# Placing eight batches of scan states on the 128 partitions: two row layouts for broadcast DMAs

## The chip, the cores and the metric

The kernel runs on one core of one Trainium2 chip. The metric is the device time of one execution in microseconds, the median over repeated runs. The core has five engines that follow their own instruction streams: TensorE (PE in the profile, with its weight loads as PEld), VectorE (DVE), ScalarE (ACT), GpSimd (POOL) and SyncE (SP). SP does no arithmetic here; it issues every DMA of the kernel. The transfers themselves are done by 16 DMA engines, which the core's queues share.

## The reference, cut to what matters

Input x is 8 batches of 1024 positions of 512 channels. Two residual layers follow each other: a modulated attention with 16 heads, and a gated state-space scan. Only the scan is touched. With 1024 inner channels, 16 states per batch and position t, it computes

```
xr, gate = split(x @ W_in.T);  xc = silu(conv4(xr + t_emb));  xn = layernorm(xc) * ln_g + ln_b
Bm, Cm, dt = split(xn @ W_xproj.T);  dt = tanh(dt @ W_dt.T + b_dt) * 0.01
ad = 1 + dt * (-tanh(A_log));  bd = Bm * min(norm(xn), 1)
h[b, n, :] = clip(h[b, n, :] * ad[b, n] + bd[b, n] * xn[b, t, :], -10, 10)      # for each t
y[b, t, :] = sum over n of Cm[b, n] * h[b, n, :]
out = x + ((y + D * xn) * silu(gate)) @ W_out.T
```

The state h is therefore 8 x 16 = 128 rows of 1024 channels: one row per partition. At each position all 16 rows of a batch need the same vector xn[b, t, :].

## The kernel before, in words

The attention fills the first 3.5 ms and hands its result to the scan through DRAM. The scan takes positions in 32 chunks of 32 (`TC`), each made of two tiles of 16 positions (`TT`). In a tile the 128 partitions hold (position, batch) pairs for the layer norm; for the recurrence the 128 partitions hold (state, batch) pairs. The change of layout is a round trip through DRAM, on the SP queue:

- `spill` (L622) writes the normalised tile `xt`, 128 x 1024, to a DRAM tile `xd`, 512 KB, ordered so that the 4 positions x 1024 channels that one batch needs next lie together, 16 KB. Its DRAM side has the shape 4 x 32 x 1024, its SBUF side 128 x 1024.
- `fetch` (L765) reads back four positions at a time. For each of the eight batches it issues one DMA that reads one 16 KB piece and writes it to that batch's 16 partitions, `xb[rows(b)]`: eight broadcasts of 256 KB, 2 MB in all, per four positions. The tiles `xb` have three buffers of four positions.
- `rows(b)` (L514) says which partitions those are. Before, batch b has the partitions 64*(b//4) + b%4 + 4n for the states n = 0 to 15: batches 0 to 3 lie interleaved in partitions 0 to 63, batches 4 to 7 in partitions 64 to 127. The broadcasts are issued in the order 0, 4, 1, 5, 2, 6, 3, 7, which alternates between the halves.

`spread` (L665) uses the same `rows(b)` for eight small DMAs per chunk that bring the recurrence's coefficients from 16 partitions to 128 (`bca`). The rest of the recurrence is one instruction per position and engine: ACT multiplies `xb` by a column of weights (`weigh`, L779, in place), DVE adds it to the state and saturates (`step`, L802, tile `h`, six buffers), and after four positions PE forms the outputs with the matrices `yw` (`products`, L784). `yw` is the coefficient times `mask_y`, which is 1 where a partition belongs to a batch; that matrix and the columns `b_dt` and `a_log` are laid out on the host.

Everything is issued in an order written out by hand. `at(n, f, ...)` puts a piece of work at step n, where one step is one position; at every step the recurrence comes first and then the pieces in the order in which they were put there. For chunk c, with p0 = 32(c-1), the first tile's spill stands at step p0+17 and the second's at p0+21; `skip` (L636), which multiplies `xt` in place and so must wait until the spill has read it, stands at p0+20 and p0+26. `fetch(g)` stands at step 4g-9, `weigh(n)` two steps ahead of position n, `products(g)` at 4g+4. All engines work their streams in order. SP also waits in order: each DMA carries one of eight semaphores in turn, so that a DMA is issued only once the one eight places ahead of it has landed.

Also on the SP queue in each chunk: a load of `x1` (512 KB, L435) and eight stores of the output (`out_send`, L755, 64 KB each, whose DRAM side is 4 x 8 x 512).

Of the kernel before, what the change touches and what calls it, by code (L numbers as in the profile page):

```python
# [15 lines left out]
P = 128  # L16
B = 8
# [6 lines left out]
NS = 16  # L24
TC = 32
TT = 16
EPS = 1e-5
EPS_DM = 1e-8


@with_exitstack
def modulated_attention(ctx, tc, const, x1_d, xu_d, S, x, xT, cond, wT, ident, sT):
# [80 lines left out]
    with tc.tile_pool(name="w0", bufs=2) as wp:  # L113
        s2T = wp.tile([P, 2 * KH, B], F32, name="s2T")
        nc.scalar.activation(s2T, sT, AF.Square)
        for n, name in enumerate(NAMES):
# [5 lines left out]
            for o in range(KH):  # L122
                for k in range(KH):
# [6 lines left out]
                    )  # L130
            nc.vector.tensor_scalar_add(dc[:, n], d_ps, EPS_DM)
        nc.scalar.activation(dc, dc, AF.Sqrt)
# [266 lines left out]
def gated_scan(ctx, tc, const, x1_d, S, w_in, w_conv, cols, ln_g, ln_b, w_x, w_xd, w_dt, b_dt, a_log,  # L399
# [113 lines left out]

    def rows(b):  # L514

        r0 = 64 * (b // 4) + b % 4
        return slice(r0, r0 + 4 * (NS - 1) + 1, 4)

    def by_rows(ap):

# [144 lines left out]
    def spread(st):  # L665
        st["bca"] = one.tile([P, 3, TC], F32, name="bca")
        for b in range(B):
            nc.sync.dma_start(out=st["bca"][rows(b)], in_=xp[:, :, b, :])
# [96 lines left out]
    def fetch(g):  # L765

        c, t = divmod(4 * g, TC)
        i, q = divmod(t // 4, TT // 4)
        xb = xbp.tile([P, 4, DI], F32, name="xb")
        for b in (0, 4, 1, 5, 2, 6, 3, 7):  # L770
            src = sts[c]["xd", i].rearrange("(q b) r c -> q b (r c)", q=4)[q, b]
            nc.sync.dma_start(  # L772
                out=xb[rows(b)].rearrange("p r c -> p (r c)"),
                in_=src.unsqueeze(0).to_broadcast([NS, 4 * DI]),
            )
        for r in range(4):
            xbs[4 * g + r] = xb[:, r]
# [86 lines left out]
    for g in range(S // 4):  # L864
        at(4 * g - 9, fetch, g)
        at(4 * g + 4, products, g)
# [99 lines left out]
```

## Time and profile before

| what | us |
| --- | --- |
| median of 3 runs (6273.12 to 6277.6) | 6274.84 |
| the profiled execution's own time | 6262.97 |
| its span in the profile | 6261.2 |
| scan, from the first broadcast to the last state | about 3536 to 6240 |
| PE busy in the stretch 3560 to 6240 | 2447.53 of 2680 |
| DVE busy there | 2243.25 |
| ACT busy there | 1912.92 |
| mean busy share of the 16 DMA engines there | 0.82 |
| data moved there | 224 GB/s |

PE's busy time counts pipelined matmuls with modelled ends. The DMA share is the mean over 16 engines, so it can hide that a few of them carry more than the rest. One chunk of 32 positions takes 2680/32 = 83.75 us. The attention before it is not touched by the change.

### The profile page before, as it was taken

What the parts mean: (1) busy time and instruction counts of PE and PEld (TensorE: products, weight loads), DVE (VectorE), ACT (ScalarE), POOL (GpSimd) and SP (SyncE); (2) the same over time, 40 slices, a digit from 0 to 9 for tenths busy, and PEclk for the clock granted to TensorE, in tenths of its full rate; (3) what the DMA queues carried; (4) which work ended last, traced back from release to release, by engine and by line L of the source; (5) the groups of instructions that cost most, each with busy time, mean ns of one, the idle gap of its engine ahead of it and who ended that gap; (6) DMA issues with size and microseconds to landing.
All of it is one profiled execution on the core that took longest, in us unless ns stands there. A gap on an engine that the chain in (4) does not pass through costs nothing.

```text
span 6261.2 us, 112973 instructions
## 1 busy us (share of the span) xinstructions
PE 5796.5 (93%) x42960; PEld 3314.5 (53%) x42960; DVE 4484.0 (72%) x6917; ACT 3843.8 (61%) x6743; POOL 1266.2 (20%) x1156
## 2 busy tenths in 40 slices
PE   7999999999999999999999699999999999999998
PEld 5555555655555555555555444444444444444443
DVE  2666666656667666666665488888888888888887
ACT  3555655655556556555554477777777777677675
POOL 2433433434334334343332000000000000000000
PEclk8999999999999999999999899999999999999999
DMA  2112111112121111121211678888888888888787
GB/s 70 35 30 71 30 55 49 35 48 67 30 70 31 55 48 35 48 67 30 55 28 55 177 224 223 221 221 228 225 223 227 222 222 228 220 224 226 221 223 198
DMA packets 396859, 781.65 MB, mean 125 GB/s; under 512 B 196496, under 2 KB 295056, under 8 KB 363552
## 3 DMA queue, kind: packets, MB, share of 16 engines
q1 hardware_dynamic: 396320, 774.44, 45.4%
q8 instruction: 341, 5.59, 0.4%
q14 instruction: 198, 1.62, 0.1%
HBM read 663.62 MB, written 83.89 MB: 119 GB/s over the span
## 4 chain that ended last, share of the span: by engine, by line
PE 60%; DMA 14%; DVE 10%; ACT 8%; SPq 5%; issue 3%; POOL 0%; DVEq 0%; ACTq 0%; POOLq 0%
PE mm_ps L153 16%; PE t_ps L262 13%; PE s_ps L252 9%; DMA xb<-xd 8%; PE mm_ps L269 8%; DVE h L806 5%; DMA xd<-xt 4%; PE o_ps L745 4%; SPq L772 4%; PE in_ps L547 4%; ACT pr L370 3%; PE y_ps L793 3%; ACT pT L367 1%; PE g_ps L705 1%; PE in_ps L551 1%
## 5 line engine op out<-in xcount | busy, mean ns | idle before, releaser
L360 DVE TENSOR_REDUCE nmax<-s_ps 128x1 f32<-128x1024 f32 x1024 | 1206.2, 1220 | 478.0 <-PE s_ps L255 477.4
L806 DVE CUSTOM_DVE_ANT_0 h<-h,xb,lim 128x1024 f32<-128x1024 f32 x1024 | 1374.7, 1342 | 209.7 <-PE y_ps L793 71.7
L367 ACT COPY pT<-t_ps 128x512 f32<-128x512 f32 x1024 | 549.8, 589 | 1378.8 <-PE t_ps L262 1378.5
L262 PEld LDWEIGHTS t_ps<-ident,pr 128*128 128x128 f32 x8192 | 909.7, 141 | 646.4 <-issue 453.2
L782 ACT ACTIVATE xb<-xb,ws 128x1024 f32<-128x1024 f32 x1024 | 1135.9, 1145 | 62.4 <-DVE ws L682 31.3
L370 ACT ACTIVATE pr<-s_ps,nmax 128x1024 f32<-128x1024 f32 x1024 | 1139.6, 1127 | 6.1 <-DVE nmax L360 5.7
L262 PE MATMUL t_ps<-ident,pr 128*128 128x128 f32 x8192 | 1096.1, 277 | 30.7 <-ACT pT L367 28.5
L793 PE MATMUL y_ps<-h,yw 128*32 128x512 f32 x4096 | 675.5, 617 | 159.7 <-DVE h L806 159.6
L252 PE MATMUL s_ps<-kT,qT 32*128 32x512 f32 x2048 | 601.1, 641 | 4.4 <-ACT pr L370 4.4
L389 POOL TENSOR_SCALAR pr<-pr,rinv 128x1024 f32<-128x1024 f32 x512 | 572.6, 1118 | 145.6 <-DVE rinv L388 142.9
L255 PE MATMUL s_ps<-k,q 32*128 32x512 f32 x2048 | 578.2, 640 | 0.0
L269 PEld LDWEIGHTS mm_ps<-pT,vt 128*32 128x32 f32 x16384 | 438.0, 110 | 235.1 <-issue 94.3
L705 PE MATMUL g_ps<-win,x1t 128*128 128x512 f32 x1024 | 508.5, 643 | 58.1 <-ACT sq_ps L631 51.3
L269 PE MATMUL mm_ps<-pT,vt 128*32 128x128 f32 x16384 | 517.6, 274 | 47.5 <-ACT vt L200 18.5
L547 PE MATMUL in_ps<-x,win 128*128 128x256 f32 x2048 | 490.9, 383 | 28.9 <-ACT xt L733 17.4
L375 POOL TENSOR_SCALAR pr<-pr,rinv 128x1024 f32<-128x1024 f32 x256 | 286.5, 1119 | 1109.5 <-PE t_ps L262 741.0
L547 PEld LDWEIGHTS in_ps<-x,win 128*128 128x128 f32 x2048 | 389.8, 192 | 152.4 <-issue 71.6
L384 POOL TENSOR_SCALAR pr<-pr,rinv 128x1024 f32<-128x1024 f32 x256 | 286.3, 1118 | 882.6 <-DVE rinv L383 855.8
L745 PE MATMUL o_ps<-wout,xt 128*128 128x512 f32 x1024 | 463.7, 596 | 0.7 <-ACT xt L733 0.7
L793 PEld LDWEIGHTS y_ps<-h,yw 128*32 128x32 f32 x4096 | 133.9, 110 | 545.6 <-DVE h L806 295.0
L381 DVE COPY pT<-t_ps 128x512 f32<-128x512 f32 x512 | 352.2, 688 | 77.2 <-PE t_ps L262 76.8
L705 PEld LDWEIGHTS g_ps<-win,x1t 128*128 128x128 f32 x1024 | 198.2, 204 | 384.6 <-issue 229.5
(129 smaller groups left out, 6750.7 us busy)
## 6 DMA issues: line engine op xcount, KB each, us to landing
xb<-xd SPq DMA_DIRECT2D x2048, 256.0 KB
xd<-xt SPq DMA_DIRECT2D x64, 512.0 KB
xq<-in_x SPq DMA_DIRECT2D x16, 1024.0 KB
q<-qT SPq DMA_DIRECT2D x128, 128.0 KB
xr<-in_xT SPq DMA_DIRECT2D x64, 256.0 KB
xu_d<-xr SPq DMA_DIRECT2D x64, 256.0 KB
xr<-xu_d SPq DMA_DIRECT2D x64, 256.0 KB
x_d<-xr SPq DMA_DIRECT2D x64, 256.0 KB
```

What stands on the lines that cost most here:

```text
L153: nc.tensor.matmul(ps, w, x, start=(k == 0), stop=(k == KH - 1))
L252: nc.tensor.matmul(s_ps[i][:, 0:HW], st["q"][r, qc], st["k"][r, 0:HW], start=True, stop=True)
L262: nc.tensor.transpose(ps[:, j], pr[:, c0 : c0 + P], ident)
L269: nc.tensor.matmul(av[r], vt[:, kt, r], pT[:, i, kt], start=(kt == 0), stop=(kt == KT - 1), skip_group_check=True,)
L360: nc.vector.tensor_reduce(nmax[i], s_ps[i], AX.X, ALU.max, negate=True)
L370: nc.scalar.activation(fresh[i], s_ps[i], AF.Exp, bias=nmax[i], accum_out=rsum[i])
L547: nc.tensor.matmul(ps, win_sb[:, kk, k * P : (k + 1) * P], st["x1"][:, kk].rearrange("p b t -> p (b t)"), start=(kk == 0), stop=False,)
L705: nc.tensor.matmul(ps, st["xo", i][:, k], win_sb[:, k, DI + half * 512 : DI + (half + 1) * 512], start=(k == 0), stop=(k == KH - 1),)
L745: nc.tensor.matmul(ps, st["gT", i][:, k, :], wout_sb[:, k, :], start=False, stop=(k == KI - 1), skip_group_check=True,)
L782: nc.scalar.mul(xbs[n], xbs[n], sts[c]["ws"][:, t : t + 1])
L793: nc.tensor.matmul(st["y", i][32 * r : 32 * r + 32, hf * 512 : (hf + 1) * 512], yws[i][:, 4 * q + r, :], hs[4 * g + r][:, hf * 512 : (hf + ...
L806: nc.vector._custom_dve(dve_ops.TENSOR_ADD_SAT, out=h, in0=last["h"], in1=xbs.pop(n), s0=lim[:, 0, t : t + 1], s1=lim[:, 1, t : t + 1],)
```

## The change

The partitions of a batch are given by a new function. Batches 0 to 3 now have the partitions 32 + b + 4n, that is the middle half 32 to 95, four batches interleaved. Batches 4 and 5 have b%2 + 2n, the first quarter 0 to 31, two batches interleaved; batches 6 and 7 have 96 + b%2 + 2n, the last quarter 96 to 127. The order in which the eight broadcasts of a group are issued becomes 4, 6, 0, 1, 5, 7, 2, 3. The host lays out `mask_y`, `b_dt` and `a_log` by the same function.

```diff
+def state_rows(b):
+
+    if b < B // 2:
+        return 32 + b, 4
+    return 96 * (b // 6) + b % 2, 2
...
     def rows(b):
 
-        r0 = 64 * (b // 4) + b % 4
-        return slice(r0, r0 + 4 * (NS - 1) + 1, 4)
+        r0, d = state_rows(b)
+        return slice(r0, r0 + d * (NS - 1) + 1, d)
...
-        for b in (0, 4, 1, 5, 2, 6, 3, 7):
+        for b in (4, 6, 0, 1, 5, 7, 2, 3):
...
-    mask_y = np.broadcast_to(
-        np.eye(B, dtype=np.float32).reshape(2, 1, 4, B), (2, NS, 4, B)
-    ).reshape(P, B)
+    batch_of, state_of = np.zeros(P, int), np.zeros(P, int)
+    for b in range(B):
+        r0, d = state_rows(b)
+        batch_of[r0 + d * np.arange(NS)] = b
+        state_of[r0 + d * np.arange(NS)] = np.arange(NS)
+    mask_y = np.eye(B, dtype=np.float32)[batch_of]
...
     def rows(v):
-        return np.tile(np.repeat(np.asarray(v), 4), 2)[:, None]
+        return np.asarray(v)[state_of][:, None]
```

The number of instructions, their order on each engine, their sizes and what each waits for stay as they are.

## The prediction

> **What bounds the kernel now.** I began with the page's slices, which split the run at about 3.5 ms into attention and scan.
>
> ```profile
> DMA  2112111112121111121211678888888888888787
> GB/s 70 35 30 71 30 55 49 35 48 67 30 70 31 55 48 35 48 67 30 55 28 55 177 224 223 221 221 228 225 223 227 222 222 228 220 224 226 221 223 198
> ```
>
> In the scan the DMA engines are busy for eight tenths. Only the scan uses the changed rows, so the first 3.5 ms cannot move. Next, the chain of waits over the scan alone (3555 to 6240 us), by line:
>
> ```profile
> by line: DMA xb<-xd 18.7%; DVE h L806 11.8%; DMA xd<-xt 9.5%; PE o_ps L745 9.5%; SPq L772 8.5%; PE in_ps L547 7.9%; PE y_ps L793 6.4%; issue 4.4%; PE g_ps L705 2.8%; PE o_ps L739 1.9%; PE in_ps L551 1.9%; ACT xb L782 1.9%; DVE xt L605 1.7%;
> ```
>
> Broadcasts in flight hold 18.7% of 2685 us = 502 us of the chain, spills in flight 9.5% = 255 us. Then the list of waits over 3560 to 6240, for what the lateness does:
>
> ```profile
> ACT sq_ps L631 <- DVE xt L620: 238.0, 32, 8.8
> ...
> PE y_ps L793 <- DVE h L806: 159.6, 105, 3.1
> ...
> DVE xt L637 <- DMA xd<-xt: 127.4, 58, 4.3
> ...
> DVE h L806 <- ACT xb L782: 55.2, 67, 2.7
> ...
> PE g_ps L705 <- ACT sq_ps L631: 51.3, 28, 3.7
> ```
>
> DVE stands 127 us on spills, since `skip` may not overwrite `xt` before the spill has read it; behind it in DVE's order stand the scaling (L620) and the states. PE then waits 160 us for states and 51 us for the squares behind L620. PE idles 2680 - 2447.53 = 232 us in the scan, mostly for a late DVE. That is the most that any faster transfer can give.
>
> Last, how fast transfers run by the partitions that they write, from five short stretches. The last two columns are the DMA share and GB/s.
>
> ```profile
> 679.10:680.10 1.00, 1.00 (x9) 1.00 (x10) 0.57 (x3) 0.77 (x3) 0.00 (x0) 1.00 0.95 207
> 3471.00:3473.00 2.00, 0.00 (x0) 0.00 (x0) 0.00 (x0) 0.00 (x0) 0.00 (x0) 0.50 1.01 416
> 3480.00:3481.50 1.50, 0.00 (x0) 0.00 (x0) 0.00 (x0) 0.00 (x0) 0.00 (x0) 0.50 1.00 399
> 5009.00:5013.00 4.00, 4.00 (x13) 2.17 (x12) 4.00 (x5) 2.71 (x4) 0.00 (x0) 1.00 0.99 266
> 5130.00:5130.80 0.80, 0.80 (x5) 0.17 (x1) 0.25 (x1) 0.00 (x0) 0.00 (x0) 0.50 0.25 102
> ```
>
> Row 1 is a copy of 64 partitions to the other 64 in the attention (L177, L178): every DMA engine busy, 207/0.95 = 218 GB/s. Row 2 is the load of `win` to 128 partitions, 416/1.01 = 412. Row 3 is mostly the broadcasts of layer-norm rows and D to 128 partitions: one 4 KB source read 128 times, yet 399. Row 4 is a stretch of nothing but broadcasts to `xb`: 266/0.99 = 269. Row 5 is a spill alone: a quarter of the engines, 102 GB/s.
>
> [...]
>
> [...]
>
> **The change part by part.** Sizes from the issue list: a broadcast has 256 KB = 262144 B.
>
> *Broadcasts now.* 262144/269 = 0.975 us each; eight make 7.80 us, and a chunk of eight groups 62.4 us on each engine. Engines 0 to 3 add two spills of 524288/102 = 5.14 us each, eight output stores of eight 2 KB pieces per engine (84 ns each in the packet records, 0.67 us a store), and the `x1` load of 524288/412 = 1.3 us: 62.4 + 10.3 + 5.4 + 1.3 = 79.4 us of 83.75, 95%. The other twelve carry 63.7 us. The mean, (4 x 79.4 + 12 x 63.7)/16 = 67.6, is 0.81 of a chunk, against the 0.82 measured: the working holds. Four DMA engines are thus the fullest resource, above PE's 91%.
>
> *Broadcasts after.* Batches 0 to 3: 262144/412 = 0.636 us. For 4 to 7 the trace has no case [...]: at best they go as now (0.975; they still come in pairs from both sides, 4-6 and 5-7), at worst as row 1 (1.20). Eight cost 2.54 + 3.90 = 6.44 us, or 7.35 us. I take 6.44: the alternation that gives 269 is kept. That is -1.36 us per group (-17%), with -0.45 us (-6%) as the weak end. Engines 0 to 3 fall to 68.5 us, 82%, per chunk.
>
> *What of it lies on the path.* Pieces of broadcast flight on the chain are 6.0 us long on average, so 502/6.0 = 84 of them. About 2.0 us is fixed (at the scan's first broadcast 1.35 us from issue to the first packet, and 0.65 us from a packet's end to its semaphore); 4.0 us is queue. At 17% that saves 0.7 us; engines at 82% instead of 95% also keep a shorter queue, for which I add 0.3 as an estimate. 84 x 1.0 = 84 us. Spill pieces average 10.26 us, 255/10.26 = 25: 2.0 fixed, 5.14 own transfer, unchanged, and 3.1 behind the group issued just ahead. Taking a third of that, 1.1, gives 25 x 1.1 = 28 us. Together 112 us. A quarter I count as taken over by what is late next and sees no DMA: DVE waiting for PE at the states (72 us) and at the statistics (71 us). That leaves -84 us.
>
> *At no cost.* The order of the eight issues: as many, each about 0.63 us of SP; a batch issued first isn't used earlier, since `weigh` reads all 128 partitions and waits for the last. The small `bca` DMAs (6 KB) change partitions only; they stand under `decay` three steps (8 us) later, and if that cover were gone their eight issues would cost 5 us a chunk, as before. `mask_y` and columns: host layout, same loads. No wait is added; `skip`, and DVE's work behind it, keeps the same wait for an earlier landing.
>
> Sum: 6262.97 - 84 = 6179 for the profiled execution; the shown runs lie 12 us above it, hence 6274.84 - 84 = about 6190.
>
> **The rivals.**
>
> *Slower: engines 0 to 3 collide with each other.* [...] with only four engines in a broadcast, packets took 0.61 us. [...] 32 x 0.636 + 32 x 1.20 = 58.8 us; if one packet in eight then takes 1.8, 63 us or more, above today's 62.4. It decides once their mean packet passes 0.975 us. At +0.3 us for 84 pieces: +25 us, 6300. Against: with twelve engines active, packets cluster near 0.92 us, 12 x 16 KB at 213 GB/s, not at 0.61 for four and 1.20 for eight. The half seems to be shared evenly.
>
> *No change: the source is the limit.* 269 could be what sixteen readers of one DRAM piece get. Then it stays at 6275. Row 3 speaks against it (one source, 399), and row 1 shows the half's limit with no DRAM at all.
>
> *Small gain: the weak end.* 7.35 us per group, or PE and DVE taking over most: -20 to -50 us, about 6240.
>
> *Large gain: the queue drains.* If spills find no queue (25 x 3.1 = 78 us) and broadcasts lose 1.5 us (126 us), less a quarter: -150 us, about 6125; PE's 232 us of idle is the wall.
>
> **How the numbers follow.** Forecast (6155 to 6225) 0.40, small gain 0.18, large gain 0.15, slower 0.15, no change 0.12. The range 6110 to 6285 leaves out most of the slower case and the far end of the large gain. What a measurement of this kernel can tell from no change is 0.2%, 12.5 us: faster 0.71, same 0.15, slower 0.14; a little of the small gain and of the slower case falls into the middle. Those that are faster have their own range of 6110 to 6245.
>
> **What would show it.** The DMA share in the scan falls from 0.82 to about 0.72 (by 17% of 62.4 us in a chunk, over a chunk shorter by 84/32 = 2.6 us); a stretch of broadcasts alone rises from 266 to above 310 GB/s; `skip`'s wait for the spill falls from 127 us to under 80; PE's idle in the scan falls from 232 us towards 150; the attention stays. If the share falls and the waits for spills and broadcasts do not, the collision on engines 0 to 3 is real. [...] I am wrong most easily in the step from transfer rate to landing: a DMA lands when its slowest engine does.

## The result and the profile after

The changed kernel takes 6290.06 us (median of 15 runs, 6278.62 to 6302.24) against 6273.12 us before (15 runs, 6267.69 to 6282.96): 1.0026 times as long, 95% interval 1.0019 to 1.0033. It is slower by 17 us, where 84 us less had been forecast; 6290 lies just above the stated range of 6110 to 6285.

The slices of the page after, for the DMA engines:

```profile
DMA  2112111112121121121112688888878788888877
GB/s 69 36 28 66 35 55 48 35 48 67 31 71 28 55 55 28 51 64 37 48 30 61 182 219 222 215 215 230 222 224 227 224 220 223 225 226 223 222 224 185
```

Nothing of the forecast is to be seen: still eight tenths busy, still about 223 GB/s. By the windows over 3560 to 6240 us the share is 0.83; 0.82 before, 0.72 forecast. Three short stretches at a full share, at 3637, 3806 and 3892 us, ran at 250, 277 and 296 GB/s, where more than 310 had been forecast, and PE's idle time went from 232 to 242 us instead of towards 150. The chain of waits over the scan after, by line:

```profile
by line: DMA xb<-xd 21.0%; DVE h L813 11.2%; DMA xd<-xt 10.2%; PE o_ps L752 8.8%; SPq L779 8.1%; PE in_ps L554 7.4%; PE y_ps L800 6.1%; issue 4.3%; PE g_ps L712 2.9%; ACT xb L789 1.9%; PE o_ps L746 1.8%; PE in_ps L558 1.8%; DVE xt L612 1.6%
```

Broadcasts in flight went from 18.7% to 21.0% of the scan's chain, spills from 9.5% to 10.2%. The list of waits after, over 3560 to 6240 (us in total, times, longest):

```profile
ACT sq_ps L638 <- DVE xt L627: 248.2, 31, 13.7
...
PE y_ps L800 <- DVE h L813: 161.4, 104, 3.1
DVE xt L644 <- DMA xd<-xt: 152.3, 60, 9.9
...
PE g_ps L712 <- ACT sq_ps L638: 59.1, 29, 6.9
...
DVE h L813 <- ACT xb L789: 54.9, 71, 3.4
```

`skip` waits 152 us for the spill instead of 127, its longest wait 9.9 us instead of 4.3; PE behind it waits 59 us for the squares instead of 51. ACT, too, waits longer for broadcasts at `weigh`, first before and then after:

```profile
ACT xb L782 <- DMA xb<-xd: 23.1, 11, 4.6
```

```profile
ACT xb L789 <- DMA xb<-xd: 48.9, 20, 4.7
```

DVE's wait for ACT at the states stayed at 55 us, so this second delay did not show there. The same list for SP's queue, first before and then after, shows the wait for the transfer eight places ahead (in the trace before, each of 2625 issues of the scan ended at least 0.49 us after that one's last semaphore update):

```profile
SPq L772 <- DMA xb<-xd: 95.9, 219, 2.0
```

```profile
SPq L779 <- DMA xb<-xd: 170.6, 313, 2.0
```

SP waits for a broadcast to land 313 times instead of 219 and 75 us longer in all. In the chain of waits, followed through windows of 60 us from 3600 to 6180, a piece of broadcast flight lasts 6.3 us on average (77 pieces) instead of 5.9 (76), and a piece of spill flight 10.2 us as before (27 and 25 pieces). So broadcasts landed later on the path. The packet records show how the DMA share can stay while they do. Over 3700 to 6100 us, the 16 KB packets of the broadcasts took

| | mean ns | 5% | 25% | 50% | 75% | 95% |
| --- | --- | --- | --- | --- | --- | --- |
| before | 974 | 646 | 932 | 1011 | 1041 | 1112 |
| after | 976 | 615 | 812 | 995 | 1112 | 1356 |

The mean is the same. A quarter of the packets became clearly faster, and as much was lost on others. A broadcast has landed with the last of its semaphore's 16 updates; the time from the first to the last was 1.44 us before and 2.36 us after (medians over the scan). The slow packets became slower: their 95% went from 1.112 to 1.356 us.

### The profile page after: what moved, and what is told of

It is laid out like the page before. It is cut to its first block, busy times and chain, and to the rows that moved or that the text cites. A ratio compares the mean times of both kernels' runs of the same rounds, so it can differ in the third digit from the quotient of the medians.

```text
span 6285.1 us, 112973 instructions
## 1 busy us (share of the span) xinstructions
PE 5808.0 (92%) x42960; PEld 3315.1 (53%) x42960; DVE 4482.9 (71%) x6917; ACT 3846.3 (61%) x6743; POOL 1265.8 (20%) x1156
## 4 chain that ended last, share of the span: by engine, by line
PE 59%; DMA 16%; DVE 10%; ACT 8%; SPq 4%; issue 3%; POOL 0%; DVEq 0%; ACTq 0%; POOLq 0%
PE mm_ps L160 15%; PE t_ps L269 13%; DMA xb<-xd 9%; PE s_ps L259 9%; PE mm_ps L276 8%; DVE h L813 5%; DMA xd<-xt 5%; PE o_ps L752 4%; SPq L779 4%; PE in_ps L554 3%; ACT pr L377 3%; PE y_ps L800 3%; ACT pT L374 1%; PE g_ps L712 1%; PE in_ps L558 1%
```

## The experiments

Two theories were tested. The first: the partitions that a transfer writes decide its rate, and the changed rows lose again when transfers to different partitions meet, above all when the DMA engines that carry other work lag behind. The rival: sixteen readers of one DRAM piece are the limit, whatever the partitions. The ratios below are against the kernel before on the same chip.

In the recorded texts, engines 0 to 3 is a name for the four that carry spills and stores; no record numbers an engine. In the trace before, over 3700 to 6100 us, four of a spill's 4 KB packets run at once in 84% of the time that any does, and four of the stores' 2 KB packets in 66%. That the same four carry both is my estimate; of 7296 store packets none began while a spill packet ran.

### The rates by themselves: m_rates

A kernel of DMAs alone. `gate()` begins each stretch when the one before has landed.

```
def send(k, b, rows, j):
    r0, d = rows(b)
    nc.sync.dma_start(out=ts[k][slice(r0, r0 + d * (NS - 1) + 1, d)],
                      in_=x[j].unsqueeze(0).to_broadcast([NS, N]))
...
for p in (p_half_only, p_before, p_middle_only, p_quarter_only, p_quarters, p_after, p_step8, p_one):
    gate()
    p()
```

> Leaves out the whole computation: only broadcasts of 16 KB pieces of x from DRAM to 16 partitions each, 256 KB per transfer, in eight stretches, each begun when the one before has landed. [...] first half alone about 1.20 us per transfer (218 GB/s); alternating halves about 0.98 (269); middle half alone about 0.64 (412, as fast as SP issues); first quarter alone 1.20; the two quarters in turn about 0.98; the changed order as a whole 0.81 if a middle transfer costs 0.64 and an outer one 0.98, and more if transfers collide across; step 8 [...] about 0.98 as the alternation before, but 0.64 if the limit belongs to the half; one transfer of 2 MB to all 128 partitions 0.64 per 256 KB. If the one source that 16 engines read at once is the limit: about 0.98 in every stretch.

The windows of its eight stretches, in that order (last columns: DMA share, GB/s):

```profile
57.00:119.00 62.00, 0.81 (x7) 0.00 (x0) 1.00 0.95 201
122.00:223.00 101.00, 0.00 (x0) 0.00 (x0) 1.00 1.01 249
230.00:259.00 29.00, 0.00 (x0) 0.00 (x0) 1.00 0.99 400
267.00:296.00 29.00, 0.00 (x0) 0.00 (x0) 1.00 1.01 204
303.00:356.00 53.00, 0.00 (x0) 0.00 (x0) 1.00 1.02 232
363.00:455.00 92.00, 0.76 (x7) 0.00 (x0) 1.00 0.97 271
459.00:575.00 116.00, 2.67 (x24) 0.00 (x0) 1.00 0.97 228
577.00:620.00 43.00, 0.00 (x0) 0.00 (x0) 1.00 1.02 219
```

Row 3 ends the rival: 16 engines read one piece at once at 400 GB/s when they write to the middle half (partitions 32 to 95, step 4). One half alone (row 1) and one quarter alone (row 4) give half of that at a full share. Per packet: half 1.229 us, alternating halves 1.045, middle 0.643 (0.611 for most), quarter 1.263, two quarters in turn 1.126, step 8 1.088.

Two terms of my sum come out here. Step 8 uses both halves in every transfer, yet costs 1.088 and not 0.61. From the twelve-engine packets I had argued that the engines of a half share its limit evenly; this contradicts it. And row 6, the changed order as a whole, takes 0.921 per packet, not 0.81. By position in the order 4, 6, 0, 1, 5, 7, 2, 3, the mean packets are 0.90, 1.11, 0.97, 0.70, 0.90, 1.11, 0.97, 0.71 us. (The records name no engine; the packets were sorted into 16 chains, each packet starting within a few ns of the end of the one before it.) A middle transfer that follows a pair of outer ones isn't cheap: it costs 0.97, and only the second one, at 0.70, is near its own price. What slows the first is not shown. On average the outer four cost 1.00 and the middle four 0.84.

Row 8 was not expected: one DMA of 2 MB to all 128 partitions, with the source repeated 16 times, goes at 219 GB/s.

### The parts in the kernel: rows_old_order, step8, half_after_half

```diff
# rows_old_order, from the changed kernel
-        for b in (4, 6, 0, 1, 5, 7, 2, 3):
+        for b in (0, 4, 1, 5, 2, 6, 3, 7):
# step8, from the changed kernel, with the order of before too
-    if b < B // 2:
-        return 32 + b, 4
-    return 96 * (b // 6) + b % 2, 2
+    return b, 8
# half_after_half, from the kernel before
-        for b in (0, 4, 1, 5, 2, 6, 3, 7):
+        for b in (0, 1, 2, 3, 4, 5, 6, 7):
```

> The changed rows with the order of issue from before, so that middle and outer transfers take turns. [...] between -0.3% and +0.5% of before, and different from the changed kernel, since each outer transfer now runs beside a middle one. Source decides: as before, within 0.1%.

> Batch b on partitions b + 8n, order of issue as before: every transfer uses both halves[...]. [...] as before within 0.3% [...]. A limit per half: transfers at 0.64 us, about 80 us faster. Source decides: as before.

> Rows of before, but the broadcasts in the order 0 to 7, four to one half and then four to the other. [...] packets go from 0.975 us towards the 1.22 of one half alone; at 1.15 engines 0 to 3 carry 64 x 1.15 + 17 = 91 us a chunk, more than the chunk's 84, so the time rises by 150 to 350 us. If the rate of the broadcasts is not what sets the pace: less than 30 us.

Measured: rows with the old order 6373.78 us, ratio 1.0167 (1.0153 to 1.0181); step 8 6284.26 us, 1.0027 (1.0016 to 1.0037); half after half 6467.24 us, 1.032 (1.0302 to 1.0337). Packets took 1.047, 1.017 and 1.124 us on average. The order alone is worth 3.2% with the rows of before and 1.4% (1.0167 against 1.0026) with the changed ones, with the same bytes and issues. The waits of the rows with the old order and then of half after half, over 3560 to 6240, show more on the same path:

```profile
DVE xt L644 <- DMA xd<-xt: 225.9, 59, 9.3
...
ACT xb L789 <- DMA xb<-xd: 122.8, 51, 5.2
```

```profile
DVE xt L637 <- DMA xd<-xt: 289.1, 57, 10.0
...
ACT xb L782 <- DMA xb<-xd: 147.1, 63, 4.8
```

So the forecast's frame stands: the rates of broadcasts do reach the time, and the waits of `skip` for the spill and of `weigh` grow with them. The mean and the tail are not the whole account: step 8 lost as much as the changed kernel with a higher mean, 1.017 us, and a short tail, 95% at 1.119 us. The two halves of the change belong together: the new rows without the new order lose 1.67%. My expectation for it reached to +0.5% only; where middle and outer transfers take turns, every one meets another kind.

### Who lags: m_lag and m_lag2

The same broadcasts, 96 per stretch, with the kernel's other transfers put between the groups of eight: a 512 KB spill, on four DMA engines, and stores of 64 KB, also on four.

```
for k in range(12):
    for b in order:
        send(k, b, rows, 8 * k + b)
    if k % 4 == 1 and spill:
        spill()
    if k % 4 == 3 and store:
        store()
```

> Leaves out the whole computation: broadcasts as in the kernel, 96 per stretch, in nine stretches: rows and order of before, changed rows and order, changed rows with the old order; each first alone, then with a 512 KB spill on four DMA engines and four stores of 64 KB, also on four engines, after every fourth group, then the same with the spill on 16 engines. Lagging engines collide (theory): alone about 1.05, 0.92 and, for the old order, 1.0 us per packet; with the four-engine work the changed rows lose most of their lead, 0.97 or more against 1.0, and the stretch ends no earlier than that of before or within 3% of it; with the spill on 16 engines the lead comes back in part. If the lead is lost for another reason (the engines of the compute side, the small transfers): the changed rows keep their lead of about 12% in all three.

| 16 KB packets, mean us (length of the stretch) | rows and order of before | changed rows and order | changed rows, old order |
| --- | --- | --- | --- |
| alone | 0.922 (89.6) | 0.891 (86.9) | 1.110 (108.6) |
| spill and stores on four engines | 0.997 (114.4) | 1.055 (122.3) | 0.973 (114.9) |
| spill on 16, stores on four | 0.988 (105.5) | 1.055 (113.2) | 1.082 (117.6) |

Alone, the changed rows lead. With the work on four engines, the stretch takes 122.3 us against 114.4, 7% longer. That the lead is lost is as the theory has it; that the spill on 16 engines brings nothing back is not. Nor does the third column fit it: with the spill on four engines and the stores, the changed rows in the old order became faster, 0.973 us instead of 1.110. m_lag2 takes the additions one at a time.

> Leaves out the whole computation: twelve stretches of 96 broadcasts, in turn with the rows and order of before and with the changed ones: alone; with a spill on four DMA engines after every fourth group; with four stores on four engines instead; with a spill on all 16 engines; with a 512 KB load to 128 partitions, also on 16; alone again. If it is work on four engines alone that costs the changed rows their lead: ahead (0.89 to 0.92 us per packet against 0.92 to 1.05) when alone and with both kinds of 16-engine work, behind (1.02 or more against about 1.0) with the spill on four engines and with the stores. If any work between the groups does it: behind in all four. The two stretches alone at the end show how far a stretch repeats.

Its windows, in turn before and changed: alone, spill on four, stores on four, spill on 16, load to 128 partitions, alone again.

```profile
58.00:155.00 97.00, 0.00 (x0) 0.00 (x0) 1.00 1.01 257
162.00:247.00 85.00, 0.00 (x0) 0.00 (x0) 1.00 1.01 290
255.00:360.00 105.00, 0.00 (x0) 0.00 (x0) 1.00 0.93 248
368.00:470.00 102.00, 0.00 (x0) 0.00 (x0) 1.00 0.91 257
478.00:583.00 105.00, 0.00 (x0) 0.00 (x0) 1.00 0.98 242
592.00:701.00 109.00, 0.00 (x0) 0.00 (x0) 1.00 0.97 233
709.00:797.00 88.00, 0.00 (x0) 0.00 (x0) 1.00 1.01 298
805.00:894.00 89.00, 0.00 (x0) 0.00 (x0) 1.00 1.01 292
902.00:1006.00 104.00, 0.00 (x0) 0.00 (x0) 1.00 1.02 253
1015.00:1104.00 89.00, 0.00 (x0) 0.00 (x0) 1.00 1.01 292
1112.00:1217.00 105.00, 0.00 (x0) 0.00 (x0) 1.00 1.01 236
1225.00:1312.00 87.00, 1.29 (x13) 0.00 (x0) 1.00 1.02 307
```

The rates include the added bytes. With the spill whole, on four engines, the DMA share falls to 0.93 and 0.91, and with the stores to 0.98 and 0.97; with the spill cut in four it stays at 1.01. By that share the texts count the cut spill as one on 16 engines. Packets took, before against changed: alone 1.011 and 0.898; spill on four 0.985 and 0.935; stores on four 1.056 and 1.083; spill on 16 0.890 and 0.904; load 1.049 and 0.908; alone again 1.107 and 0.885. Only the stores put the changed rows clearly behind, with a 95% value of 1.51 us against 1.13; the spill on four engines, which I had expected to do it too, left them ahead. With the spill on 16 the two are about level, on account of the rows of before, which became fast.

### The spill on 16 engines: before_spill16, after_spill16

```diff
-        nc.sync.dma_start(out=st["xd", i].rearrange("n r c -> r n c"), in_=st["xt", i])
+        for r in range(4):
+            nc.sync.dma_start(out=st["xd", i][:, r, :], in_=st["xt", i][32 * r : 32 * r + 32])
```

> Rows and order of before; the spill is cut in four transfers of 32 partitions [...] so that all 16 DMA engines carry it. If engines 0 to 3 are the full ones: their load falls from 79 to about 72 us of a chunk's 84, a spill's own 5.1 us falls to about 1.3, DVE's wait for the spill (127 us) nearly goes, and the time falls by 60 to 110 us in spite of six more issues a chunk (3.8 us of SP). If the chain through the spill is not what sets the pace: less than 15 us.

> The changed kernel with the spill cut in four transfers of 32 partitions, on all 16 DMA engines. If the changed rows lose because four engines lag behind and collide: the lead of the rows comes back, packets at about 0.92 us, time 0.979 to 0.983 of before, at or below the 0.983 of the rows of before with the same spill. If they lose in any case: 0.985 to 0.988, that is 0.3% above it.

Rows of before: 6160.98 us, 0.983 (0.9816 to 0.9843), which beats both kernels by 1.7 and 2%. Changed rows: 6164.48 us, 0.9837 (0.9822 to 0.9851), the same within the intervals. The wait of `skip`, rows of before and then changed rows, over 3560 to 6140:

```profile
DVE xt L638 <- DMA xd<-xt: 2.9, 2, 1.9
```

```profile
DVE xt L645 <- DMA xd<-xt: 2.8, 5, 1.6
```

127 us became 3 us. The broadcasts' packets did not become faster (0.975 and 0.967 us): what fell is the wait for the spill. Whether that is its own shorter transfer or the lighter load on the four engines that carried it, this run does not separate. The changed rows' extra 17 us is not seen once the spill no longer holds DVE; a lead they do not gain either.

### The stores left out: before_spill16_nostore, after_spill16_nostore, before_nostore, after_nostore

```diff
         o_sb = st.pop("o_sb")
+        if c < NCH - 1:
+            return
```

The first two have the spill on 16 engines as well.

> Rows of before, spill on 16 engines, and the stores of the output left out except in the last chunk, so that most of the output is not written and no DMA works on four engines alone. Packets stay near 0.975 us; the time falls a little below the 0.983 of before that the spill on 16 engines gives, to 0.975 to 0.983.

> The same with the changed rows and order. If work on four engines alone costs the changed rows their lead: packets at 0.93 us or less, and the time as with the rows of before or up to 0.5% below it. If any work between the groups costs it: packets at 0.96 to 0.98 as with the stores, and no gain.

> The kernel before with the stores of the output left out except in the last chunk (most of the output is not written); the spill stays on four engines. Engines 0 to 3 lose 5.4 us a chunk, so 0.990 to 1.000 of before; packets about 0.98 us.

> The changed kernel with the same stores left out. If the stores on four engines are what turns the changed rows into a loss: packets at 0.95 us or less, and the time at or below that of the rows of before without stores, by 0 to 0.5%. If something else does: still 0.2 to 0.4% above it, packets no better than its 0.98.

| | rows of before | changed rows |
| --- | --- | --- |
| spill on 16, no stores: ratio | 0.9832 (0.9816 to 0.9848) | 0.9827 (0.9812 to 0.9841) |
| its packets, mean and 95%, us | 0.989, 1.082 | 0.933, 1.228 |
| no stores, spill on four: ratio | 0.9992 (0.9985 to 0.9999) | 0.9973 (0.9962 to 0.9983) |
| its packets, mean and 95%, us | 0.985, 1.096 | 0.952, 1.286 |

In all four variants most of the output is not written. The last pair settles the sign. Without the stores and with nothing else touched, the changed kernel is faster than the kernel before in the same form, 6253.27 us against 6265.67, and their intervals do not overlap. `skip`'s wait, from the lists over 3560 to 6230, first rows of before without stores and then changed rows without stores:

```profile
DVE xt L637 <- DMA xd<-xt: 99.7, 31, 5.9
```

```profile
DVE xt L644 <- DMA xd<-xt: 86.6, 32, 5.9
```

With the stores it was 127 against 152. So the stores, 0.5 MB of about 18 MB moved in a chunk, decide between a gain of 12 us and a loss of 17. Which property of them does it is not shown: they use four engines, move 2 KB pieces (84 ns each) and take places in SP's queue, and no variant carried them on 16 engines. `skip`'s wait tells the direction here, not the size: for the rows of before it fell by 28 us and the time by 0.08%. With the spill on 16 and no stores the packets of the changed rows lead by 0.056 us and the time does not follow: there the rate of the broadcasts no longer decides.

## Why the prediction was wrong

*The fullest resource and the path.* The path was right: `skip`'s wait for the spill rose or fell with the time in every pair shown, and shortening the spill took 104 us off at once. That four engines, filled to 95% of a chunk, are the limit was not confirmed. The 95% is an estimate, since no record gives the load of one engine, and taking the stores' estimated 5.4 us a chunk off what it took for the same engines changed the time of the kernel before by only 0.08%.

*The cost of the broadcasts after, 6.44 us for eight.* This is the step that failed. It priced each transfer as if among its own kind. A middle one stood at 0.636: that it would go at the 412 GB/s of the load to 128 partitions was my estimate. It is right alone (0.643), but is 0.84 on average in the changed order, because a middle transfer beside an outer one is not at its own price (0.97). The outer ones, put at 0.975, are 1.00 in that order; that the trace had no case of them had been said. In isolation eight cost 8 x 0.921 = 7.4 us, the weak end that I had named; in the kernel, with the stores, 8 x 0.976 = 7.8 us, no gain. Apart from the rival below, the forecast had no term for what the kernel's other transfers do to the rate of the changed rows.

*From rate to landing.* I took the saving per transfer as the saving in landing, and named this as the easiest place to be wrong. At an equal mean packet a broadcast on the chain landed 0.35 us later, where 1.0 us earlier had been forecast, and the 95% packet went from 1.112 to 1.356 us. That the one caused the other is argued; it fits, but no run changed the tail alone.

*The rival on the slower side.* It had the direction and the size (+25 us forecast, +17 measured). Its 1.20 us for half of the broadcasts and 1.8 us for one packet in eight were estimates. That the numbers are so close is luck as long as the mechanism is not shown. It made engines 0 to 3 each other's obstacle. Whether those four or all 16 become slower stays open: where the spill or the stores interrupt the stream of packets, the records can't be sorted by engine reliably. I gave it 0.15 because twelve-engine packets near 0.92 seemed to say that a half is shared evenly; step 8, at 1.088, says that it is not.

*The source as the limit.* Excluded, as argued: 400 GB/s from one piece.

What makes transfers to the middle and to the outer quarters slow each other is not shown. Open, too, are why the old order on the changed rows became faster with the other work (from 1.110 to 0.973 us a packet), and why 64 KB stores do more to the changed rows than a 512 KB spill (1.083 us against 0.935). Shown are the rates, the tails, and that the stores turn the sign.

## What to carry to other kernels

Price a transfer in the company that it will have, and look at the tail of its packets as well as the mean: in the changed kernel a broadcast's last semaphore update came 2.36 us after its first (median), 1.44 us before the change. Before moving destinations, count how many DMA engines each transfer uses: a spill alone showed a share of 0.25, and cutting it in four took 104 us off the kernel, six times what the layout moved. A layout that leads in isolation (0.89 to 0.92 us per packet against 0.92 to 1.11) can lose its lead to a few small transfers in between, so try it among the transfers that it will meet.

## What was not expected of the hardware

- The stretch of alternating halves alone took 1.045, 0.922, 1.011 and 1.107 us per packet in four tries in three programs on three chips, almost constant within each try; the last two are of one program on one chip. The changed order alone took 0.921, 0.891, 0.898 and 0.885. Why is not shown.
- One 2 MB DMA to 128 partitions with a 16-fold repeated source ran at 219 GB/s, while the load of `win` to 128 partitions ran at 416. Writing to all 128 partitions was not enough; what else decides, no run shows.
- Leaving out all stores on the kernel before gave 0.9992 of the time, though they are an estimated 5.4 us a chunk on the engines that the prediction took for the fullest.
